# A table that moves 40 operations in the planned issue order of a two-stage conditioned block, and four PSUM banks for the last quarter turned by TensorE

## The chip, the core and the metric

The kernel runs on one core of one Trainium2 chip. The metric is the device time of one launch in microseconds (us). TensorE is called PE in the profile, its weight loads PEld, VectorE is DVE, ScalarE is ACT, GpSimd is POOL and SyncE is SP; here they are named either way.

## The reference, cut to what matters

`x` has 2 x 2048 tokens of 512 features, all in float32. A condition vector gives six modulation vectors, which scale and shift two normalisations and gate two branches:

```python
emb = silu(t) @ ada_w + ada_b
shift_msa, scale_msa, gate_msa, shift_mlp, scale_mlp, gate_mlp = split(emb, 6)
h = gelu((_ln(x) * (1 + scale_msa) + shift_msa) @ ssm_w1 + ssm_b1)        # 512 -> 512, exact gelu
x = x + gate_msa * (h @ ssm_w2 + ssm_b2)                                  # 512 -> 512
hf = gelu((_ln(x) * (1 + scale_mlp) + shift_mlp) @ ff_w1 + ff_b1)         # 512 -> 1024, tanh gelu
return x + gate_mlp * (hf @ ff_w2 + ff_b2)                                # 1024 -> 512
```

## The kernel before

**Tiles and stages.** The 4096 tokens are cut into eight blocks of 512 (`TB`). Each block goes through `norm1`, `ssm1`, `ssm2` and `norm2`; the last of these sends the normalised tokens, turned so that features lie on partitions, through DRAM (`turned_d`). Then four pairs of blocks go through the two products of the second branch, `up` (stage names "ff1 0" to "ff1 3") and `down` ("ff2 0" to "ff2 3").

**Fewer multiplications.** Each product is done by a scheme with seven multiplications of halves instead of eight, with sums of operands made beforehand (`first`, `second`) and sums of results behind. `up` and `down` use it twice, one inside the other: seven outer products of seven inner ones, so 49 multiplications, called leaves here. A leaf of `down` is two matmuls with 256 columns, and each of these is two records of the trace, so a leaf is four. The price of fewer matmuls is adds: operand sums between SBUF tiles on VectorE or GpSimd (`parts` calls `tt("vg", ...)`, line 258), and results added out of PSUM on VectorE (line 258 too, or `scaled_add`, line 1049).

**Banks.** PSUM has eight banks. Inside one inner product the leaves run in the order P1, P5, P6, P2, P7, P3, P4 (`CARRIED`). P1, P6, P7 and P4 write into one bank in turn, so P7 can't begin before VectorE has read what P6 left there. Two inner products are interleaved, leaf by leaf, so there are three other leaves between P6 and P7 of one product.

**What sets the order.** Nothing is issued while the functions run. Each operation is recorded with `Plan.add` (line 67): the engines that may do it (`engs`, where "vg" lets VectorE or GpSimd do it), an assumed cost, and in `shared` the engines on which it takes what the planner treats as one shared lock, a port between SBUF and these two engines. An add between SBUF tiles takes it on either engine; an add with a PSUM operand takes it on GpSimd only; copies, transposes and statistics of VectorE don't take it. `Plan.order` (line 89) works out by when each result is due if TensorE is never to wait, and `simulate` (line 113) runs a list schedule: of the operations that could start now on an engine the one that is due first is taken, and where several engines could start at the same time the one that is due first goes. The kernel then issues everything in the order of the simulated starts, so each engine's instructions stand in a fixed order in the program.

**Port waits.** Where the simulation shows that GpSimd was ready, but VectorE held the lock, the GpSimd operation gets `after` (lines 180 and 181), and line 1405 turns this into a real dependency: on the chip GpSimd then waits until that VectorE operation has ended. It is the planner's way to let an urgent VectorE add go first.

**DMAs.** All are issued by SP's queue, some by ScalarE's. They take eight completion semaphores in turn, in the order of issue, so that a DMA can't be issued before the eighth one ahead of it has landed.

**The end.** The last two outer products of the last pair finish two quarters of the output. TensorE turns them back to token rows (`turned_by_pe`, line 1187): for each of four parts of a quarter two transposes go into a PSUM bank (line 306), VectorE adds the kept input out of that bank (line 1201), and a DMA writes the part out. `TURNED_AT` (line 1184) gives each half `h` of a quarter `blk` a bank; the two parts `e` of a half share it.

Of the kernel before, what the change touches and what calls it, by code (L numbers as in the profile page):

```python
# [13 lines left out]
EPS = 1e-06  # L14


class Op:
    __slots__ = ("n", "engs", "fn", "cost", "lat", "shared", "size", "lead", "care", "after", "done", "sooner", "deps", "succ", "late", "on", "start", "end", "note")


class Plan:
# [67 lines left out]
    def order(self):  # L89
        ops = self.ops  # L90
        for op in ops:
            if op.engs == "p":
                op.deps = {d for d in op.deps if ops[d].engs != "p"}
            for d in op.deps:
                ops[d].succ.append(op.n)
        t, due = 0.0, {}
        for op in ops:
            if op.engs == "p":
                due[op.n] = t
                t += op.cost["p"]  # L100
        due.update((n, t + late) for n, late in self.closing)
        for _ in range(2):
            for op in reversed(ops):
                late = due.get(op.n, 1e9)
                for s in op.succ:
                    late = min(late, ops[s].late - (1 + op.care) * (self.HOP + min(op.lat.values()) + op.size / self.RATE))
                op.late = late - op.sooner
            self.simulate()
            wait = ops[self.anchor].start - due[self.anchor]
            due = {n: t + wait for n, t in due.items()}  # L110
        return sorted(ops, key=lambda op: (op.start, op.n))

    def simulate(self):
        ops, hop = self.ops, self.HOP
# [86 lines left out]
def kernel(  # L201
# [51 lines left out]
    def tt(e, o, a, b, f):  # L253
        n, ps = cols(o), in_psum(a, b)
        cost = {"v": n / 0.96 + 70, "g": 2.12 * n + 145}
        plan.add(
            e,
            lambda E: E.tensor_tensor(o, a, b, f),  # L258
            [o],
            [a, b],  # L260
            cost,
            {"v": cost["v"] + 85, "g": cost["g"] + 45},
            "g" if ps else "vg",
        )
# [38 lines left out]
    def turn_by_pe(o, a, identity, start, stop):  # L303
        plan.add(
            "p",
            lambda E: E.matmul(o, a, identity, start=start, stop=stop, is_transpose=True, skip_group_check=True),  # L306
            [o],
            [a, identity],
            {"p": 120.0},
            {"p": 290.0},  # L310
        )

    def dma(o, a, q="s", lead=0.0, lat=2000.0, sooner=0.0):
        size = max(cols(o.unsqueeze(0)), 1) * 4
        outs = [o] if o.tensor.name in scratch else []
        ins = [a] if a.tensor.name in scratch else []
        lead = lead or (0.0 if ins or not outs or size <= plan.LITTLE else 25000.0)
        plan.add(q, lambda E: E.dma_start(out=o, in_=a), outs, ins, {q: plan.ISSUE}, {q: lat}, size=size, lead=lead)
        plan.ops[-1].sooner = sooner
# [24 lines left out]
    def kb(t, at, n):  # L344
        return t[:, at * 256 : (at + n) * 256]

    def cut(t, form, **sizes):
        return t.rearrange(form, **sizes)
# [5 lines left out]
    banks = []  # L354
# [40 lines left out]
    ident = kb(far_r, 24, 1)[:, :P]  # L395
# [548 lines left out]
    summed = cut(rows_r, "p (r e t) -> p r e t", r=4, e=2)  # L944
# [115 lines left out]
    def rest_in(s, d, blk, x):  # L1060
        half = slice(d * D // 2, (d + 1) * D // 2)
        dma(x, x1_d[2 * s + blk][:, :, half])
        return x, out_blk[2 * s + blk][:, :, half]
# [117 lines left out]

        return sums, last_sum, prepare, leaf

    TURNED_AT = ((3, 4), (2, 0))
    tail, waiting, leaves_read = [{}, {}], [], [0]

    def turned_by_pe(blk, r, f, quad):
        got = tail[blk]
        if not got:
            got["x"], got["out"] = rest_in(NBLK // 2 - 1, 1, blk, cut(kb(hidden_r, 8 * blk, 4), "p (c d) -> p c d", c=C))  # L1190

        def turned_back():
            e, h = int(quad[0]) - 1, int(quad[1]) - 1
            bank = cut(banks[TURNED_AT[blk][h]], "p (c e d) -> p c e d", c=2, e=2)
            for c in range(2):
                col = slice((2 * h + c) * P, (2 * h + c + 1) * P)
                turn_by_pe(bank[:, c, e], summed[:, r, e, col], ident, c == 0 and h not in got, c == 1)
            got[h] = True
            c, d = slice(2 * h, 2 * h + 2), slice(e * P, (e + 1) * P)
            x = got["x"][:, c, d]  # L1200
            tt("v", x, bank[:, :, e], x, ALU.add)
            dma(got["out"][:, c, d], x, "sa"[e])
            plan.closing.append((plan.ops[-1].n, 3000.0))

        n = leaves_read[0] = leaves_read[0] + 1
        if f in ("P7", "P2", "P3", "P4"):
            waiting.append((n, turned_back))
        done = blk == 0 and f == "P4"
        while waiting and (done or waiting[0][0] + 2 <= n):
            waiting.pop(0)[1]()  # L1210
# [190 lines left out]
    behind = mybir.DependencyInfo(mybir.DependencyClass.Sync, mybir.DependencyReason.DATA)  # L1401
# [49 lines left out]
```

## Time and profile before

| | |
|---|---|
| time, median of 3 runs | 562.89 us (562.89, 562.89, 564.47) |
| the profiled execution: its own time / its span | 563.11 us / 561.3 us |
| PE busy | 552.9 us, 98% of the span |
| PEld busy | 481.7 us, 86% |
| DVE busy | 479.2 us, 85% |
| POOL busy | 385.0 us, 69% |
| ACT busy | 282.9 us, 50% |
| granted TensorE clock | 0.998 |
| HBM traffic | 217 GB/s over the span |

The span runs from the first instruction of the program to the last end. In rows of a timeline the first number is the start in us from there, the second the duration, then engine, line of the source, operation, output and inputs, the shape, and a count where equal neighbours are merged; in brackets stands how long the engine had been idle and what ended that. Lines 296 and 306 are the matmul and the transpose of TensorE; 258 is every add. Since one helper records all adds, tiles tell them apart: `rows<-bank,rows` adds a leaf's result out of PSUM, `far`, `near`, `hidden`, `turned`, `fw` are regions of SBUF that hold operands and their sums.

### The profile page before, as it was taken

The numbers are of one execution on the slowest core, as the hardware profiler recorded it, in microseconds if no ns is written. First come the engines' busy times: TensorE is split into PE (matmuls) and PEld (weight loads), VectorE is DVE, ScalarE is ACT, GpSimd is POOL, SyncE is SP. The second block draws the span as 40 slices with busy tenths as digits, with TensorE's granted clock in tenths as the row PEclk, the third lists the DMA queues.
The fourth block names the chain that finished last, engine by engine and source line by source line (L and its number), as shares of the span: only waits on it lengthen the run. The fifth ranks groups of instructions, "written<-read, shape, count | busy, mean of one in ns | idle before, by whom it ended". The sixth has DMA issues, their size and how long they took to land.

```text
span 561.3 us, 8747 instructions
## 1 busy us (share of the span) xinstructions
PE 552.9 (98%) x2809; PEld 481.7 (86%) x2809; DVE 479.2 (85%) x848; ACT 282.9 (50%) x523; POOL 385.0 (69%) x475
## 2 busy tenths in 40 slices
PE   8999999999999999999999999999999999999995
PEld 4888889888898988888888888888888888888884
DVE  5696888888779578899999997789988989998987
ACT  3473866674877844666205347414247414244230
POOL 2887747979946299985646868676767766547581
PEclk9999999999999999999999999999999999999999
DMA  8963799988399978995201999611998612983417
GB/s 313 398 229 82 233 363 309 316 259 269 106 276 327 291 311 249 330 292 171 57 20 38 286 322 301 226 39 45 303 325 286 212 39 67 312 288 122 140 45 218
DMA packets 66945, 123.68 MB, mean 220 GB/s; under 512 B 5668, under 2 KB 34260, under 8 KB 65364
## 3 DMA queue, kind: packets, MB, share of 16 engines
q1 hardware_dynamic: 64080, 121.27, 65.9%
q10 hardware_dynamic: 2820, 1.86, 1.3%
q8 instruction: 22, 0.36, 0.3%
q14 instruction: 23, 0.19, 0.1%
HBM read 77.89 MB, written 44.18 MB: 217 GB/s over the span
## 4 chain that ended last, share of the span: by engine, by line
PE 91%; DVE 6%; DMA 2%; POOL 0%; issue 0%; DVEq 0%; POOLq 0%
PE bank L296 90%; DVE rows L258 2%; DVE near L258 1%; DMA fw<-in_L_cond_ada_w_dram 1%; DVE far L258 1%; PE bank L306 1%; DVE fw L258 1%; DVE hidden L258 0%; DMA fw<-in_L_cond_ada_b_dram 0%; DVE far L1073 0%; POOL far L258 0%; POOL fw L258 0%; POOL rows L258 0%; DVE turned L660 0%; DVE rows L1049 0%
## 5 line engine op out<-in xcount | busy, mean ns | idle before, releaser
L296 PE MATMUL bank<-turned,ring 128*128 128x256 f32 x896 | 210.2, 380 | 0.2 <-DVE turned L660 0.2
L296 PEld LDWEIGHTS bank<-turned,ring 128*128 128x128 f32 x896 | 168.0, 190 | 23.1 <-DVE turned L660 0.4
L258 DVE TENSOR_TENSOR hidden<-bank,hidden 128x512 f32<-128x512 f32 (+2 forms) x178 | 126.4, 738 | 23.9 <-PE bank L296 19.9
L296 PE MATMUL bank<-near,hidden 128*128 128x256 f32 (+1 forms) x470 | 95.1, 350 | 0.0
L296 PEld LDWEIGHTS bank<-near,hidden 128*128 128x128 f32 x470 | 82.2, 191 | 9.3 <-POOL near L258 0.3
L296 PE MATMUL bank<-far,fw 128*128 128x256 f32 (+1 forms) x354 | 86.0, 374 | 0.2
L258 POOL TENSOR_TENSOR turned<-turned 128x512 f32<-128x512 f32 (+1 forms) x62 | 70.4, 1148 | 20.4 <-DVE turned L258 9.0
L296 PE MATMUL bank<-ring 128*128 128x256 f32 x336 | 82.4, 380 | 0.0
L258 DVE TENSOR_TENSOR rows<-bank,rows 128x256 f32<-128x256 f32 (+1 forms) x142 | 66.1, 478 | 16.0 <-PE bank L296 11.9
L296 PEld LDWEIGHTS bank<-far,fw 128*128 128x128 f32 x354 | 66.5, 190 | 9.6 <-issue 0.5
L296 PEld LDWEIGHTS bank<-ring 128*128 128x128 f32 x336 | 63.7, 190 | 9.0 <-issue 0.5
L285 ACT COPY bank<-bank 128x512 f32<-128x512 f32 (+2 forms) x84 | 37.7, 449 | 63.0 <-PE bank L296 62.2
L276 ACT ACTIVATE hidden<-hidden,cols 128x512 f32<-128x512 f32 (+1 forms) x66 | 44.7, 710 | 42.9 <-DVE hidden L258 42.9
L258 POOL TENSOR_TENSOR hidden<-hidden 128x128 f32<-128x128 f32 (+2 forms) x45 | 43.5, 976 | 25.3 <-DVE hidden L258 13.1
L296 PE MATMUL bank<-near,fw 128*128 128x256 f32 (+1 forms) x246 | 60.7, 377 | 0.0
L296 PE MATMUL bank<-hidden,fw 128*128 128x256 f32 (+1 forms) x216 | 53.3, 376 | 0.4 <-DVE rows L258 0.4
L296 PEld LDWEIGHTS bank<-near,fw 128*128 128x128 f32 x246 | 46.1, 190 | 6.4 <-issue 0.2
L276 ACT ACTIVATE turned<-turned,mod,mod 128x512 f32<-128x512 f32 x56 | 42.2, 807 | 9.0 <-DMA turned<-turned 8.4
L296 PEld LDWEIGHTS bank<-hidden,fw 128*128 128x128 f32 x216 | 40.3, 190 | 6.5 <-DVE rows L258 0.8
L258 POOL TENSOR_TENSOR ring<-turned,ring 128x256 f32<-128x256 f32 x42 | 30.6, 740 | 20.7 <-PE bank L296 17.0
L276 ACT ACTIVATE rows<-rows,gb,mod 128x512 f32<-128x512 f32 (+1 forms) x34 | 26.5, 787 | 34.9 <-DVE rows L258 25.0
L258 POOL TENSOR_TENSOR fw<-fw 128x256 f32<-128x256 f32 (+1 forms) x38 | 35.6, 944 | 11.8 <-DMA fw_parts<-fw 4.3
(123 smaller groups left out, 735.7 us busy)
## 6 DMA issues: line engine op xcount, KB each, us to landing
ring<-fw_parts SPq DMA_DIRECT2D x28, 512.0 KB, 4.8
turned<-far SPq DMA_DIRECT2D x52, 256.0 KB, 4.2
ring<-fw_parts SPq DMA_DIRECT2D x28, 384.0 KB, 5.2
turned<-turned SPq DMA_DIRECT2D x32, 256.0 KB, 5.4
back<-far SPq DMA_DIRECT2D x52, 128.0 KB, 2.9
rows<-back SPq DMA_DIRECT2D x13, 512.0 KB, 5.1
fw_parts<-fw SPq DMA_DIRECT2D x21, 256.0 KB, 4.6
fw<-in_L_cond_ada_w_dram SPq DMA_DIRECT2D x5, 1024.0 KB
```

The costliest lines, as they stand in the source:

```text
L258: lambda E: E.tensor_tensor(o, a, b, f),
L276: lambda E: E.activation(o, a, func, bias=bias, scale=scale),
L285: plan.add("a", lambda E: E.copy(o, a), [o], [a], {"a": cost}, {"a": cost + 60})
L296: lambda E: E.matmul(o, lhsT, rhs, start=start, stop=stop, skip_group_check=True, **kw),
L306: lambda E: E.matmul(o, a, identity, start=start, stop=stop, is_transpose=True, skip_group_check=True),
```

## The change

**A table.** `MOVED` holds 40 triples: an operation's number, an engine, and the number of the operation behind which it now stands on that engine. 32 stand on VectorE or GpSimd, five on ScalarE (two of these are DMAs) and three on SP. Ten of the operations change between VectorE and GpSimd.

**A second pass.** After the last `simulate`, a new method `in_lines` takes the five lines of operations as simulated, takes out the moved ones and puts each at its new place. Then it runs all lines strictly in order with the planner's costs, which gives new starts, and it sets every operation's `after` anew. At each step it takes the line whose head can start first; that one head is due sooner than another plays no part any more. `after` is set where, in these new starts, VectorE held the lock when GpSimd was ready.

```diff
+MOVED = (
+    (229, "v", 217), (230, "v", 242), (644, "v", 1420), (653, "v", 645), (1241, "v", 1445), (1745, "v", 1753),
...
+    (3531, "a", 3550), (3535, "a", 3527), (221, "g", 250), (646, "g", 1287), (662, "g", 1516), (2013, "g", 2301),
...
-        return sorted(ops, key=lambda op: (op.start, op.n))
+        self.in_lines()
+        return sorted(ops, key=lambda op: (op.start, op.turn))
+
+    def in_lines(self):
+        ops, moved = self.ops, {n for n, _, _ in MOVED}
+        lines = {e: [] for e in "pvags"}
+        for op in sorted(ops, key=lambda op: (op.start, op.n)):
+            if op.n not in moved:
+                lines[op.on].append(op)
+        for n, e, behind in MOVED:
+            at = next((k + 1 for k, op in enumerate(lines[e]) if op.n == behind), 0)
+            lines[e].insert(at, ops[n])
...
+        for turn in range(len(ops)):
+            soon = []
+            for e in "pavgs":
+                if at[e] < len(lines[e]) and not left[lines[e][at[e]].n]:
+                    op = lines[e][at[e]]
+                    start = max(free[e], ready[op.n], lanes[0] if op.size else lock if e in op.shared else 0.0)
+                    soon.append((start, "pavgs".index(e), e, op))
+            start, _, e, op = min(soon)
+            op.on, op.start, op.turn, op.after = e, start, turn, None
...
+            if e in op.shared:
+                if e == "g" and holder and holder.on == "v" and start > max(free_at, ready[op.n]):
+                    op.after = holder
+                lock, holder = start + op.cost[e], op
...
-    TURNED_AT = ((3, 4), (2, 0))
+    TURNED_AT = (((3, 0), (2, 4)), ((2, 2), (0, 0)))
...
-            bank = cut(banks[TURNED_AT[blk][h]], "p (c e d) -> p c e d", c=2, e=2)
+            bank = cut(banks[TURNED_AT[blk][h][e]], "p (c e d) -> p c e d", c=2, e=2)
...
-                turn_by_pe(bank[:, c, e], summed[:, r, e, col], ident, c == 0 and h not in got, c == 1)
+                turn_by_pe(bank[:, c, e], summed[:, r, e, col], ident, c == 0 and (not blk or h not in got), c == 1)
```

**The banks.** Each of the four parts of the quarter that is finished last (`blk` 0) now has a bank of its own; the other quarter keeps its two.

What the program's order shows of this follows at three places. The names are those of tiles, with numbers of PSUM banks (72 to 79); the line of every add is 258 before and 309 after, because the new code stands above it. In brackets stand the semaphores that an instruction waits for: `DVE_49` counts ends of VectorE's instructions, `PE_49`, `Pool_49` and `Activation_49` those of the others, `DMAHW0_49` to `DMAHW7_49` landings of DMAs. TensorE's order is the same up to the banks of the last two pairs of transposes.

**GpSimd in the fourth `norm2`** (`marks` are its small statistics, `fw` an operand sum of the weights of `up`, `turned` an operand sum of `norm1`). Before:

```order
L568 TENSOR_TENSOR marks_129<-marks_129 128x4 [waits Pool_49]
L569 TENSOR_SCALAR marks_129<-marks_129 128x4 [waits DVE_49,Pool_49]
L570 TENSOR_TENSOR marks_129<-marks_129 128x4 [waits DVE_49,Pool_49]
L258 TENSOR_TENSOR fw_71<-fw_71 128x256 [waits DMAHW6_49,DMAHW1_49]
L571 TENSOR_TENSOR marks_129<-marks_129 128x4 [waits Pool_49]
L572 TENSOR_SCALAR marks_129<-marks_129 128x4 [waits DVE_49,Pool_49]
L258 TENSOR_TENSOR turned<-turned 128x512 [waits DMAHW0_49,Activation_49]
L258 TENSOR_TENSOR turned<-turned 128x4x2x64 [waits DVE_49]
L258 TENSOR_TENSOR turned<-turned 128x512
L258 TENSOR_TENSOR fw_71<-fw_71 128x256 [waits DMAHW5_49]
```

and after:

```order
L619 TENSOR_TENSOR marks_129<-marks_129 128x4 [waits Pool_49]
L620 TENSOR_SCALAR marks_129<-marks_129 128x4 [waits DVE_49,Pool_49]
L621 TENSOR_TENSOR marks_129<-marks_129 128x4 [waits Pool_49]
L309 TENSOR_TENSOR fw_71<-fw_71 128x256 [waits DMAHW5_49]
L309 TENSOR_TENSOR fw_71<-fw_71 128x256 [waits DMAHW6_49,DMAHW1_49,DVE_49]
L622 TENSOR_TENSOR marks_129<-marks_129 128x4 [waits Pool_49]
L623 TENSOR_SCALAR marks_129<-marks_129 128x4 [waits Pool_49]
L309 TENSOR_TENSOR turned<-turned 128x512 [waits DMAHW0_49,Activation_49]
```

The `fw` add that waits for `DMAHW5_49` (operation 646, which overwrites what a DMA sends to `fw_parts`) stood behind three `turned` adds and now stands ahead of the last two steps of the statistics.

**VectorE in the first `down`** ("ff2 0"). Before:

```order
L258 TENSOR_TENSOR near<-hidden,near 128x1024
L258 TENSOR_TENSOR rows<-bank_78,rows 128x256 [waits PE_49]
L258 TENSOR_TENSOR rows<-bank_77,rows 128x256
L258 TENSOR_TENSOR rows<-bank_73,rows 128x256 [waits PE_49]
L258 TENSOR_TENSOR fw_71<-fw_71 128x2x128
L258 TENSOR_TENSOR near<-hidden,near 128x1024
L258 TENSOR_TENSOR rows<-bank_79,rows 128x256 [waits DVE_49,PE_49]
L258 TENSOR_TENSOR rows<-rows 128x256 [waits DVE_49]
L258 TENSOR_TENSOR rows<-bank_74,rows 128x2x256 [waits DVE_49,PE_49]
```

and after:

```order
L309 TENSOR_TENSOR near<-hidden,near 128x1024
L309 TENSOR_TENSOR far<-near,far 128x512
L309 TENSOR_TENSOR fw_71<-fw_71 128x256
L309 TENSOR_TENSOR rows<-bank_78,rows 128x256 [waits PE_49]
L309 TENSOR_TENSOR rows<-bank_77,rows 128x256
L309 TENSOR_TENSOR rows<-bank_73,rows 128x256 [waits PE_49]
L309 TENSOR_TENSOR fw_71<-fw_71 128x2x128
L309 TENSOR_TENSOR rows<-bank_79,rows 128x256 [waits DVE_49,PE_49]
L309 TENSOR_TENSOR near<-hidden,near 128x1024
L309 TENSOR_TENSOR rows<-rows 128x256 [waits DVE_49]
L309 TENSOR_TENSOR rows<-bank_74,rows 128x2x256 [waits DVE_49,PE_49]
```

One `fw` add stands earlier, and the second `near` add of 1024 elements has changed places with the read of bank 79. GpSimd's next `far<-near` add had `after` the `rows<-rows` add and now has it after the `fw_71` add of 128x2x128.

**GpSimd and VectorE in the second `down`** ("ff2 1"). GpSimd before:

```order
L258 TENSOR_TENSOR far<-hidden,far 128x512 [waits DVE_49,PE_49]
L258 TENSOR_TENSOR far<-near,far 128x512
L258 TENSOR_TENSOR near<-near 128x512 [waits Pool_49]
L258 TENSOR_TENSOR hidden<-hidden 128x1024 [waits DVE_49]
L258 TENSOR_TENSOR hidden<-hidden 128x1024 [waits DVE_49,Pool_49]
L258 TENSOR_TENSOR far<-near,far 128x512 [waits DVE_49,PE_49]
L258 TENSOR_TENSOR near<-hidden,near 128x1024 [waits DVE_49,PE_49]
L258 TENSOR_TENSOR near<-hidden,near 128x1024 [waits DVE_49]
```

and after:

```order
L309 TENSOR_TENSOR far<-hidden,far 128x512 [waits PE_49,Pool_49]
L309 TENSOR_TENSOR far<-near,far 128x512 [waits DVE_49]
L309 TENSOR_TENSOR near<-near 128x512 [waits Pool_49]
L309 TENSOR_TENSOR hidden<-hidden 128x1024
L309 TENSOR_TENSOR hidden<-hidden 128x1024 [waits DVE_49,Pool_49]
L309 TENSOR_TENSOR far<-near,far 128x512 [waits DVE_49,PE_49,Pool_49]
L309 TENSOR_TENSOR near<-hidden,near 128x1024 [waits DVE_49]
```

The first `hidden` add of 1024 elements no longer waits for VectorE, nor does the first `far` add; the second `hidden` add still does, but its `after` has gone one VectorE operation ahead (from `near<-near` to the second `far<-near,far`). One `near` add has left GpSimd. VectorE before, at the same place:

```order
L258 TENSOR_TENSOR far<-hidden 128x512 [waits Pool_49]
L258 TENSOR_TENSOR rows<-bank_74,rows 128x256 [waits DVE_49,PE_49]
L258 TENSOR_TENSOR rows<-bank_79,rows 128x256 [waits DVE_49,PE_49]
L258 TENSOR_TENSOR far<-hidden,far 128x512 [waits Pool_49]
L258 TENSOR_TENSOR rows<-bank_76,rows 128x256 [waits PE_49]
```

and after:

```order
L309 TENSOR_TENSOR far<-hidden 128x512 [waits Pool_49]
L309 TENSOR_TENSOR far<-hidden,far 128x512 [waits DVE_49,Pool_49]
L309 TENSOR_TENSOR rows<-bank_74,rows 128x256 [waits DVE_49,PE_49]
L309 TENSOR_TENSOR rows<-bank_79,rows 128x256 [waits DVE_49,PE_49]
L309 TENSOR_TENSOR rows<-bank_76,rows 128x256 [waits PE_49]
L309 TENSOR_TENSOR near<-hidden,near 128x1024
```

The `far<-hidden,far` add has gone ahead of two bank reads, and the `near` add that left GpSimd stands here. GpSimd's last `near` add has `after` the first of these rows, `far<-hidden`.

More of the change, by code (lines that the diff above doesn't have):

```diff
@@ L14 @@
 EPS = 1e-06
+MOVED = (
[7 rows of a table added]
+)
 class Op:
-    __slots__ = ("n", "engs", "fn", "cost", "lat", "shared", "size", "lead", "care", "after", "done", "sooner", "deps", "succ", "late", "on", "start", "end", "note")
+    __slots__ = ("n", "engs", "fn", "cost", "lat", "shared", "size", "lead", "care", "after", "done", "sooner", "deps", "succ", "late", "on", "start", "end", "note", "turn")
 class Plan:
@@ L110, in order @@
             due = {n: t + wait for n, t in due.items()}
-        return sorted(ops, key=lambda op: (op.start, op.n))
+        self.in_lines()
[9 more added lines that the diff above has]
+            lines[e].insert(at, ops[n])
+        left, ready = [len(op.deps) for op in ops], [0.0] * len(ops)
+        free, at = dict.fromkeys("pvags", 0.0), dict.fromkeys("pvags", 0)
+        lock, pipe, holder, lanes = 0.0, 0.0, None, [0.0] * self.LANES
+        for turn in range(len(ops)):
[7 more added lines that the diff above has]
+            op.on, op.start, op.turn, op.after = e, start, turn, None
+            free_at, free[e] = free[e], start + op.cost[e]
+            at[e] += 1
+            if op.size > self.LITTLE:
+                pipe = max(start + self.FLIGHT, pipe) + op.size / self.RATE
+                op.end = pipe + self.LANDING
+            else:
+                op.end = start + op.lat[e]
+            if op.size:
+                lanes = sorted(lanes[1:] + [op.end])
+            if e in op.shared:
+                if e == "g" and holder and holder.on == "v" and start > max(free_at, ready[op.n]):
+                    op.after = holder
+                lock, holder = start + op.cost[e], op
+            for n in op.succ:
+                gap = 0.0 if ops[n].engs == e and not op.size else self.HOP
+                ready[n] = max(ready[n], op.end + gap)
+                left[n] -= 1
     def simulate(self):
```

5 rows, old and new, of the table MOVED are left out of this document.

## Prediction

> **What bounds the kernel now.** I read the page's busy times first, then its chain, then TensorE's waits, then timelines of the stages in which the change moves something.
>
> ```profile
> PE 552.9 (98%) x2809; PEld 481.7 (86%) x2809; DVE 479.2 (85%) x848; ACT 282.9 (50%) x523; POOL 385.0 (69%) x475
> ...
> PE 91%; DVE 6%; DMA 2%; POOL 0%; issue 0%; DVEq 0%; POOLq 0%
> ```
>
> PE is busy for 98% of the span and is 91% of the chain. The matmuls don't change, so the change can only add to or take from the idle places between them. All that it can win inside is small, while a queue that now feeds PE late costs as much as it is late. So I go through the places one by one: which read of a bank or copy stands just ahead of a PE row, and how early. A leaf takes 0.86 us (rows of PE start 0.86 apart for each four matmuls), and a leaf behind a wait shows 1.10 to 1.13 instead of 1.03, so each wait costs 0.1 more.
>
> **Second `down` ("ff2 1"): two adds of GpSimd let go.** GpSimd, VectorE and PE there:
>
> ```profile
> 353.39 1.27 POOL L258 TENSOR_TENSOR far<-hidden,far 128x512 f32<-128x512 f32 x1 [1.83 <-DVE near L258]
> ...
> 355.84 1.28 POOL L258 TENSOR_TENSOR near<-near 128x512 f32<-128x512 f32 x1
> 358.95 2.36 POOL L258 TENSOR_TENSOR hidden<-hidden 128x1024 f32<-128x1024 f32 x1 [1.83 <-DVE far L258]
> 361.99 2.35 POOL L258 TENSOR_TENSOR hidden<-hidden 128x1024 f32<-128x1024 f32 x1 [0.69 <-DVE near L258]
> ```
> ```profile
> 356.65 1.02 DVE L258 TENSOR_TENSOR far<-near 128x512 f32<-128x512 f32 x1
> 357.59 1.28 DVE L258 TENSOR_TENSOR far<-near,far 128x512 f32<-128x512 f32 x2
> 358.79 0.41 DVE L258 TENSOR_TENSOR rows<-bank,rows 128x256 f32<-128x256 f32 x1
> ...
> 360.78 1.07 DVE L258 TENSOR_TENSOR near<-near 128x512 f32<-128x512 f32 x1
> 361.77 0.41 DVE L258 TENSOR_TENSOR rows<-bank,rows 128x256 f32<-128x256 f32 x1
> ...
> 363.37 1.52 DVE L258 TENSOR_TENSOR far<-hidden 128x512 f32<-128x512 f32 x1
> 364.81 0.41 DVE L258 TENSOR_TENSOR rows<-bank,rows 128x256 f32<-128x256 f32 x1
> ```
> ```profile
> 360.24 1.89 PE L296 MATMUL bank<-far,fw 128*128 128x256 f32 x8
> 361.97 2.75 PE L296 MATMUL bank<-near,fw 128*128 128x256 f32 x12
> ...
> 366.28 1.89 PE L296 MATMUL bank<-far,fw 128*128 128x256 f32 x8
> ```
>
> The rows show the lock at work. VectorE's `far<-hidden` takes 1.52 instead of some 0.65: it ends at 364.89, 0.55 after GpSimd's add (361.99 + 2.35 = 364.34). The waits in brackets are the other side: GpSimd is held until a named VectorE add has ended.
>
> The Trainium skill (page "SBUF — State Buffer", section "Who interferes with whom") says that the one that issues first has the shared pair for its whole instruction and the other is fully blocked. By it a blocked add would end a full 0.68 after GpSimd, each wait below would grow by 0.13 or so and the sum would be 565.7; the row's 0.55 speaks for a little overlap, and I go by the row.
>
> The first `hidden` add no longer waits 1.83, so it stands behind `near<-near` from 357.1. VectorE's `far<-near` is already waiting and ends at 357.67; then GpSimd has the lock until about 359.9. The first `far<-near,far` ends at 360.45 instead of 358.23, the second at 361.05, and the bank read at 361.45 instead of 359.20. The leaf into that bank is the second of the PE row of 360.24, at 361.10, and a matmul starts a little behind the read that it waits for: **0.4 late**. The second `hidden` add now follows VectorE's second `far<-near,far`, from 361.1 to 363.5, so `near<-near` ends at 364.05 instead of 361.85 and the next bank read at 364.4; its leaf is the third of the row of 361.97, at 363.69 and with the first wait (0.4 and 0.1) 364.2: **0.3 late**. Then `far<-hidden`, behind GpSimd's next add of 1.27, ends at about 365.97. At that end two instructions are let go: GpSimd's `near` add of 1024 elements (2.35) and VectorE's moved `far<-hidden,far`, which now stands ahead of the bank read of 364.81. Who is first is read from another place:
>
> ```profile
> 284.30 1.21 DVE L258 TENSOR_TENSOR near<-hidden,near 128x1024 f32<-128x1024 f32 x1
> ...
> 286.43 0.71 DVE L258 TENSOR_TENSOR fw<-fw 128x256 f32<-128x256 f32 x1
> 287.06 1.21 DVE L258 TENSOR_TENSOR near<-hidden,near 128x1024 f32<-128x1024 f32 x1
> 288.20 0.41 DVE L258 TENSOR_TENSOR rows<-bank,rows 128x256 f32<-128x256 f32 x1
> 288.64 0.43 DVE L258 TENSOR_TENSOR rows<-rows 128x256 f32<-128x256 f32 x1
> 289.18 1.02 DVE L258 TENSOR_TENSOR rows<-bank,rows 128x512 f32<-128x512 f32 x2
> ```
> ```profile
> 285.59 1.27 POOL L258 TENSOR_TENSOR hidden<-hidden 128x512 f32<-128x512 f32 x1 [2.10 <-DVE near L258]
> 289.21 1.27 POOL L258 TENSOR_TENSOR far<-near 128x512 f32<-128x512 f32 x1 [2.36 <-DVE rows L258]
> ```
> ```profile
> 290.01 1.10 PE L296 MATMUL bank<-hidden,fw 128*128 128x256 f32 x4
> 291.25 1.10 PE L296 MATMUL bank<-far,fw 128*128 128x256 f32 x4
> ...
> 293.32 2.00 PE L296 MATMUL bank<-far,fw 128*128 128x256 f32 x8
> ```
>
> GpSimd with one wait starts 0.08 after VectorE's end (285.51 to 285.59); VectorE with two waits, one for its own last instruction, 0.11 after it (289.07 to 289.18). The GpSimd add has one wait, the VectorE add two, so GpSimd is first by 0.03, until 368.4; VectorE ends at 368.95 and the read at 369.3. Its leaf is the second of the row of 366.28, at 367.15, and with 0.9 of the two waits 368.05: **1.3 late**. In all 2.0 and three times 0.1: **+2.3**. PE's rows there have no idle time now, so nothing can be won; the bounds are 0 and 2.8 (0.55 taken as 0.68, and the reads 0.1 later).
>
> **First `down` ("ff2 0"): +0.5.** The rows above. GpSimd's `far<-near` waited 2.36 for `rows<-rows`; now it follows the `fw` add that ends at 287.14, from about 287.25 to 288.52, and VectorE's `near` add of 1024, now behind the read of bank 79, ends at 289.6 instead of 288.27. `rows<-rows` ends at 290.07 and the first of the next two reads at 290.87 instead of 289.87. The leaf of 290.01 waits for it; it waits 0.18 today, and 0.87 more then. The wait ahead of 291.25 (0.38) goes, since its `fw` add stands earlier; that ahead of 293.32 (0.27) stays. So 0.87 - 0.4 = 0.5. Bounds: all three waits go, -0.8; none goes and one grows, with the third, to +1.3. I take the middle, worked out row by row.
>
> **Fourth `norm2`: +0.4.** GpSimd takes the `fw` add of operation 646 ahead of the last steps of the statistics:
>
> ```profile
> 165.55 0.73 POOL L258 TENSOR_TENSOR fw<-fw 128x256 f32<-128x256 f32 x1 [4.26 <-DMA fw_parts<-fw]
> ...
> 172.94 0.73 POOL L258 TENSOR_TENSOR fw<-fw 128x256 f32<-128x256 f32 x1
> ...
> 179.01 1.59 POOL L258 TENSOR_TENSOR fw<-fw 128x256 f32<-128x256 f32 x2
> ```
> ```profile
> 168.60 7.61 SPq L318 DMA_DIRECT2D fw_parts<-fw  x8
> ```
> ```profile
> fw_parts<-fw SPq DMA_DIRECT2D x12, 256.0 KB, 4.6
> ...
> turned<-turned SPq DMA_DIRECT2D x4, 256.0 KB, 7.1
> ```
> ```profile
> 178.88 0.38 ACT L285 COPY bank<-ring 128x256 f32<-128x256 f32 x1
> ```
> ```profile
> 180.71 0.39 PE L296 MATMUL bank<-near,hidden 128*128 128x128 f32 x2
> ```
>
> The add now waits for a DMA of SP's row of 168.60. Landing 4.6 after issue it is there at 173.2, with 7.1 at 175.7; GpSimd is at the place at 172.94, so it waits 0.2 to 2.7 and the add takes 0.8. All behind it, the statistics that ScalarE's normalisation needs among it, is 1.0 to 3.5 later. ScalarE's copy ends 1.4 ahead of the matmul at 180.71, and one ScalarE operation of 0.8 that is moved ahead fills part of its wait. What is left for PE is 0 to 1.3; by the median landing nothing, by the late one 1.3, and the add that waited 4.26 in this stage says that late ones are had: 0.4, a third of the way.
>
> The Trainium skill (page "DMA: Bandwidth & Descriptors", section "Anatomy of one DMA — SWDGE (gpsimd) path") fits 2.0 us and bytes at 436 GB/s, which would be an estimated 2.6 for 256 KB; the add would then find its data, this term would be 0 and the sum 564.8. The measured 4.6 speaks against it here, on SP's queue.
>
> **Small gains.**
>
> ```profile
> 33.03 3.10 PEld L296 LDWEIGHTS bank<-near,hidden 128*128 128x128 f32 x15 [0.27 <-POOL near L258]
> ```
> ```profile
> 460.23 1.02 DVE L258 TENSOR_TENSOR rows<-bank,rows 128x512 f32<-128x512 f32 x2 [1.22 <-POOL rows L258]
> ```
> ```profile
> 460.98 1.13 PE L296 MATMUL bank<-hidden,fw 128*128 128x256 f32 x4 [0.40 <-DVE rows L258]
> ```
> ```profile
> 555.70 0.66 PE L306 MATMUL bank<-far,rows 128*128 128x128 f32 x4 [0.69 <-DVE hidden L258]
> ```
> ```profile
> 556.18 0.76 DVE L258 TENSOR_TENSOR hidden<-bank,hidden 128x256 f32<-128x256 f32 x2 [0.53 <-PE bank L306]
> ```
>
> At 33.0 a `near` add goes to VectorE, and the wait of 0.27 with it: **-0.3**, bounds 0 and -0.4. At 460.98 the `rows<-rows` add that VectorE's read waited 1.22 for is moved from GpSimd to VectorE; of 0.40 and the longer leaf I take **-0.3**, bounds 0 and -0.6. At the end the last four transposes wait for VectorE's `hidden` add, which reads the bank that they share; with banks of their own that add and the two of 556.18 follow each other, from 555.64: 0.54 earlier, and so are the last writes: **-0.5**, bounds 0 and -0.7. The other moves stand where no PE row has idle time. Three DMAs of SP's queue and two of ScalarE's pass one to four neighbours each, at some 0.95 per issue by the row of 168.60 (7.61 for eight); what they bring is needed a whole leaf sequence later, and landings of 4.6 to 7.1 lie between, so a delay of two or three issues hides there. I cost them and the remaining adds at nothing, and 0.5 either way if that cover is gone.
>
> **The sum.** 2.3 + 0.5 + 0.4 - 0.3 - 0.3 - 0.5 = +2.1. The profiled execution took 563.1 (its span 561.3 and 1.8 around it), 0.2 above the median of 562.89. So 565.2; the terms' own spread makes it 564.6 to 566.0.
>
> **Rivals.** *A, faster:* GpSimd's first `far` add (353.39) also loses its wait of 1.83. If its short adds come over 1 us earlier, its 1024 add starts before 356.3 and is through before VectorE's adds of 357.59; then all the waits of "ff2 1" are absent, and with the gains at their best (0.8 in "ff2 0", 0.3, 0.6, 0.5, norm2 0) it is 560.9. Against it: the second `far` add now waits for VectorE's `near` add, which would itself be held by the earlier GpSimd add, so little is gained. 0.13. *B:* VectorE is first at the pair that is 0.03 apart. The 1.3 and 0.1 go: 563.8. Both gaps are of single rows; 0.17. *C:* the DMA of norm2 is late (1.3) and the wait ahead of 291.25 stays: 565.2 + 0.9 + 0.4 = 566.5. 0.13. *D:* the change does not act where I see costs, since other waits keep the old order; the three gains alone give 562.0. 0.05.
>
> **Chances.** My forecast has 0.50; 0.02 is left for gains that I don't see. The measurement can tell about 0.3%, 1.7 us, from no change, so faster means under 561.2 and slower over 564.6. Faster: A and the rest, 0.15. Same: B and D, 0.22. Slower: the forecast and C, 0.63. The range 561.6 to 566.6 takes in B, C and D, and leaves out A.
>
> **What the profile after would show.** GpSimd's two `hidden` adds of 1024 at about 357.1 and 361.1; VectorE's first `far<-near,far` 2 us long; three gaps of PE between 361 and 370, the third over 1 us; one gap of about 1 us near 290, and no wait at 33.0 nor at the last transposes; a DMA wait of GpSimd near 173. I am wrong if PE runs gapless through "ff2 1", if the third gap is missing (B), or if a gap over 0.5 us stands in a place not named here.

## The result and the profile after

The changed kernel takes 566.95 us (median of six runs, 566.19 to 569.44); the kernel before 563.20 (six runs). The ratio is 1.0074, with a 95% interval of 1.0063 to 1.0085: **3.7 us slower**, where +2.1 was forecast. The profiled execution took 568.29, its span 566.5, so it is 1.3 above the median; its gaps are read below for their places, and what a part of the change costs is taken from medians where an experiment gives one.

The page: busy times and the chain of the changed kernel.

```profile
PE 554.4 (98%) x2809; PEld 480.5 (85%) x2809; DVE 482.3 (85%) x852; ACT 283.1 (50%) x523; POOL 380.3 (67%) x471
...
PE 84%; DVE 7%; POOL 3%; issue 2%; DMA 2%; ACT 1%; DVEq 0%; POOLq 0%; ACTq 0%
```

PE's share of the chain has fallen from 91% to 84%; GpSimd and ScalarE are on it now. Since TensorE's order is the same, the start of the same PE row in both timelines says where the time went:

| row of PE starts at, before | after | after is late by | what lies between |
|---|---|---|---|
| 33.03 | 32.87 | -0.2 | the `near` add moved to VectorE |
| 177.25 | 177.42 | 0.2 | waits at 82 and 86, 0.4 in all, which no other profile shows |
| 181.60 | 183.24 | 1.6 | fourth `norm2` |
| 288.96 | 291.76 | 2.8 | waits at 205 and 216 |
| 295.15 | 298.81 | 3.7 | "ff2 0" |
| 353.33 | 356.95 | 3.6 | nothing |
| 368.01 | 374.20 | 6.2 | "ff2 1" |
| 460.98 | 466.59 | 5.6 | the `rows<-rows` add moved to VectorE |
| end of the span 561.3 | 566.5 | 5.2 | the four banks |

**"ff2 1"**, in this order GpSimd, VectorE and PE. GpSimd is no longer held, and VectorE's adds are long:

```profile
355.49 1.73 POOL L309 TENSOR_TENSOR far<-hidden,far 128x512 f32<-128x512 f32 x1
...
360.85 2.84 POOL L309 TENSOR_TENSOR hidden<-hidden 128x1024 f32<-128x1024 f32 x1
364.99 2.35 POOL L309 TENSOR_TENSOR hidden<-hidden 128x1024 f32<-128x1024 f32 x1 [1.29 <-DVE far L309]
...
369.95 2.35 POOL L309 TENSOR_TENSOR near<-hidden,near 128x1024 f32<-128x1024 f32 x1 [0.63 <-DVE far L309]
```
```profile
356.01 2.29 DVE L309 TENSOR_TENSOR near<-hidden,near 128x1024 f32<-128x1024 f32 x1
...
361.39 3.45 DVE L309 TENSOR_TENSOR far<-near,far 128x512 f32<-128x512 f32 x2
364.76 0.41 DVE L309 TENSOR_TENSOR rows<-bank,rows 128x256 f32<-128x256 f32 x1
...
369.97 2.87 DVE L309 TENSOR_TENSOR far<-hidden,far 128x512 f32<-128x512 f32 x1
372.77 1.27 DVE L309 TENSOR_TENSOR rows<-bank,rows 128x256 f32<-128x256 f32 x3
```
```profile
365.23 1.13 PE L347 MATMUL bank<-far,fw 128*128 128x256 f32 x4 [0.22 <-DVE rows L309]
...
368.37 1.10 PE L347 MATMUL bank<-near,fw 128*128 128x256 f32 x4 [0.28 <-DVE rows L309]
...
373.23 1.13 PE L347 MATMUL bank<-far,fw 128*128 128x256 f32 x4 [1.17 <-DVE rows L309]
```

Against the same rows of before PE loses 0.39, 0.44 and 1.41 there, the longer leaves aside: the three waits of the forecast. At 369.95 and 369.97 GpSimd and VectorE start 0.02 apart; GpSimd is first, and VectorE's add ends 0.54 after it (372.84 against 372.30).

**"ff2 0"**: GpSimd's add at 289.95 is 0.1 ahead of VectorE's, which so takes 2.24 instead of 1.21, and PE waits three times (rows of GpSimd, VectorE and PE).

```profile
289.95 1.27 POOL L309 TENSOR_TENSOR far<-near 128x512 f32<-128x512 f32 x1 [0.42 <-DVE fw L309]
```
```profile
290.06 2.24 DVE L309 TENSOR_TENSOR near<-hidden,near 128x1024 f32<-128x1024 f32 x1
...
292.74 1.02 DVE L309 TENSOR_TENSOR rows<-bank,rows 128x512 f32<-128x512 f32 x2
```
```profile
293.57 1.10 PE L347 MATMUL bank<-hidden,fw 128*128 128x256 f32 x4 [0.79 <-POOL fw L309]
...
296.51 1.10 PE L347 MATMUL bank<-far,fw 128*128 128x256 f32 x4
297.84 1.13 PE L347 MATMUL bank<-far,fw 128*128 128x256 f32 x4 [0.23 <-DVE far L309]
```

By the starts of its rows, the longer leaf aside, PE waits 0.95 ahead of 293.57, 0.27 ahead of 296.51, as it did before the change ahead of 293.32, and 0.39 ahead of 297.84, where it did not. The first row names GpSimd's `fw` add, but the kernel before (290.01, with the add at 291.18) and E8 start this leaf ahead of that add. What it waits for is the first of the two bank reads at 292.74 (0.69 long): it ends 0.15 ahead of the leaf, as it did before the change.

**Fourth `norm2`**: GpSimd at operation 646, then ScalarE, then PE. "Fourth" is the number in the kernel, where blocks are counted from 0 (`norm2 4`). Operation 1704 scales and shifts tokens of block 0 that come back from DRAM for `up` (`tokens 0`); it now stands ahead of the last such operation of block 7's `norm1`.

```profile
176.86 1.41 POOL L309 TENSOR_TENSOR fw<-fw 128x256 f32<-128x256 f32 x2 [3.46 <-DMA fw_parts<-fw]
```
```profile
176.55 1.52 ACT L327 ACTIVATE turned<-turned,mod,mod 128x512 f32<-128x512 f32 x2 [1.41 <-DMA turned<-turned]
178.78 0.81 ACT L327 ACTIVATE near<-fw,marks 128x512 f32<-128x512 f32 x1 [0.71 <-POOL marks L623]
...
201.67 1.52 ACT L327 ACTIVATE turned<-turned,mod,mod 128x512 f32<-128x512 f32 x2 [3.41 <-DMA turned<-turned]
```
```profile
180.04 1.99 PE L347 MATMUL bank<-turned,ring 128*128 128x256 f32 x8 [0.72 <-POOL turned L309]
182.25 0.49 PE L347 MATMUL bank<-near,hidden 128*128 128x128 f32 x2 [0.21 <-ACT bank L336]
...
206.54 8.90 PE L347 MATMUL bank<-near,hidden 128*128 128x256 f32 x40 [0.51 <-ACT bank L336]
```

GpSimd waited 3.46 for the DMA that 646 needs, more than the 2.7 taken as the most. ScalarE waited too, 1.41, at a place where it did not wait before; the first of the two operations of that row is 1704, moved ahead. PE then waits for a `turned` add of GpSimd and for ScalarE's copy, and once more at 206.54.

**The end**: PE's last six transposes run as one row, where the last four waited 0.69, and VectorE's last three adds follow each other.

```profile
560.31 1.18 PE L357 MATMUL bank<-far,rows 128*128 128x128 f32 x6
```
```profile
560.91 1.08 DVE L309 TENSOR_TENSOR hidden<-bank,hidden 128x256 f32<-128x256 f32 x3
```

### The profile page after: what moved, and what is told of

It is laid out like the page before. It is cut to its first block, busy times and chain, and to the rows that moved or that the text cites. A ratio compares the mean times of both kernels' runs of the same rounds, so it can differ in the third digit from the quotient of the medians.

```text
span 566.5 us, 8739 instructions
## 1 busy us (share of the span) xinstructions
PE 554.4 (98%) x2809; PEld 480.5 (85%) x2809; DVE 482.3 (85%) x852; ACT 283.1 (50%) x523; POOL 380.3 (67%) x471
## 4 chain that ended last, share of the span: by engine, by line
PE 84%; DVE 7%; POOL 3%; issue 2%; DMA 2%; ACT 1%; DVEq 0%; POOLq 0%; ACTq 0%
PE bank L347 84%; DVE far L309 2%; DVE rows L309 2%; DMA fw<-in_L_cond_ada_w_dram 1%; POOL turned L309 1%; DVE near L309 1%; DVE hidden L309 1%; DVE fw L309 1%; PE bank L357 1%; POOL fw L309 1%; POOL marks L611 0%; DMA fw<-in_L_cond_ada_b_dram 0%; ACT near L327 0%; DVE far L1124 0%; ACT bank L336 0%
## 5 line engine op out<-in xcount | busy, mean ns | idle before, releaser
L309 POOL TENSOR_TENSOR ring<-turned,ring 128x256 f32<-128x256 f32 x39 | 28.3, 732 | 24.0 <-PE bank L347 18.4
```

## The experiments

Each changes the one thing shown; times are medians with the ratio to the kernel before, which took 563.20 beside the first four and 563.23 beside the others.

**E1: operation 646 left in place.**

```diff
-    (221, "g", 250), (646, "g", 1287), (662, "g", 1516), (2013, "g", 2301),
+    (221, "g", 250), (662, "g", 1516), (2013, "g", 2301),
```

> The changed kernel, with operation 646 left at its old place on GpSimd, behind the turned adds. Between the two profiles PE falls 1.5 us further behind at the fourth norm2 and 1.2 us more at 204 and 213 us, and GpSimd waited 3.46 us for that operation's DMA. Theory 1 (all of this follows from that one wait): 2.7 us less than the changed kernel's 566.95, so about 564.3, and no gaps of PE at 179, 181, 205 and 216. Theory 2 (the term was sized rightly at 0.4, and the rest is another profile's luck with DMAs, or the ScalarE moves): 566.5, and the gaps at 205 and 216 stay. Theory 3 (the direct 1.5 is of 646, the later 1.2 of other moves): 565.4.

566.69 (1.0056, 1.0043 to 1.0070): nearly nothing, and theory 1 falls as it stood. PE is on time at 179 and only 0.2 late at 181, but it loses another 1.1 and 0.5 at 205 and 216. The time and these two gaps are those of theory 2, which left open whether they come from DMAs that happened to land late or from ScalarE's moves. ScalarE and GpSimd show more:

```profile
175.96 1.52 ACT L327 ACTIVATE turned<-turned,mod,mod 128x512 f32<-128x512 f32 x2 [1.58 <-DMA turned<-turned]
...
200.83 1.52 ACT L327 ACTIVATE turned<-turned,mod,mod 128x512 f32<-128x512 f32 x2 [3.75 <-DMA turned<-turned]
```
```profile
177.62 1.27 POOL L309 TENSOR_TENSOR turned<-turned 128x512 f32<-128x512 f32 x1 [1.36 <-ACT turned L327]
```

Operation 1704 waits 1.58 for a landing at the head of ScalarE's queue. Behind it stand the last `turned` of `norm1`, for which GpSimd waits, and the normalisation of the fourth `norm2`. So that block's normalised tokens still go out late. The 3.75 are not a wait for these, but for tokens of block 1 (`tokens 1`), sent out some 70 us earlier: SP's queue issues the four reads that bring them back behind the four late writes. The reads are issued 2.3 later than before, and ScalarE starts 3.2 later (200.83 against 197.66). The writes (`turned<-far`) and the reads, in the kernel before and in E1:

```profile
182.05 3.48 SPq L318 DMA_DIRECT2D turned<-far  x4
...
190.08 2.10 SPq L318 DMA_DIRECT2D turned<-turned  x4
```
```profile
185.63 3.59 SPq L369 DMA_DIRECT2D turned<-far  x4
...
192.34 2.41 SPq L369 DMA_DIRECT2D turned<-turned  x4
```

Another theory was needed: two waits side by side.

**E2: "ff2 1" as before.** Operations 2528 and 2544 back, and six of the nine port waits that the change altered there as before. Of the edit, without the lines that turn `HOLD` into dependencies:

```diff
-    ... (2303, "v", 2318), (2544, "v", 2543), (2528, "v", 2532),
+    ... (2303, "v", 2318),
...
+HOLD = {2425: 2516, 2426: 2517, 2455: 2424, 2518: 2543, 2528: 2544, 2529: 2545}
...
-            op.on, op.start, op.turn, op.after = e, start, turn, None
+            op.on, op.start, op.turn, op.after = e, start, turn, ops[HOLD[op.n]] if op.n in HOLD else None
```

> The changed kernel, with the second down as before: operations 2528 and 2544 at their old places, and GpSimd's adds there held behind the same VectorE adds as before. Theory 1 (the three waits of PE in that stage, 0.39, 0.44 and 1.41 with 0.1 each and 0.18 ahead of them, are the change's, and nothing later takes their place): 2.6 us less than 566.95, so 564.3, and PE without gaps between 358 and 374. Rival (the lateness is partly absorbed further on, or a wait downstream takes over): 565.5.

564.30 (1.0019, 1.0010 to 1.0028), 2.65 less than the changed kernel, as theory 1 has it. The rows of PE where the three waits were:

```profile
361.55 1.89 PE L347 MATMUL bank<-far,fw 128*128 128x256 f32 x8
363.28 2.75 PE L347 MATMUL bank<-near,fw 128*128 128x256 f32 x12
...
367.59 1.89 PE L347 MATMUL bank<-far,fw 128*128 128x256 f32 x8
```

No row has idle time ahead of it, and eight or twelve matmuls merge into one row, as before the change.

**E3: an empty table**, so the old order with the port waits set anew and the four banks.

```diff
 MOVED = (
-    (229, "v", 217), (230, "v", 242), (644, "v", 1420), (653, "v", 645), (1241, "v", 1445), (1745, "v", 1753),
...
 )
```

> The changed kernel with an empty table: every line of operations as before, but the port waits set anew by the second pass, and the four banks at the end. It tells the second pass apart from the moves. Theory 1 (the two hidden adds of 1024 elements that GpSimd is no longer held for cost two of the three waits in the second down; the third is the moved far add's): two gaps of about 0.4 near 361 and 364, none of 1.3, a gap of about 1 us near 290, the old waits at 33, 461 stay; 563.2 + 0.2 + 1.0 + 0.9 - 0.6 = 564.7. Rival (the port waits alone change nothing, the moves cost all): the banks' gain only, 562.6.

564.41 (1.0020, 1.0011 to 1.0030); theory 1 said 564.7. The runs lie between 564.17 and 564.75. Every engine has the order of E4, so that puts 1.7 us on the port waits set anew, with no operation moved (the order between the two DMA queues differs at five places as well). In the profiles 0.7 of it falls in "ff2 0", 0.8 in "ff2 1" and 0.25 at 392. PE in "ff2 0" and "ff2 1":

```profile
291.05 1.10 PE L347 MATMUL bank<-hidden,fw 128*128 128x256 f32 x4 [0.98 <-POOL fw L309]
...
295.20 1.13 PE L347 MATMUL bank<-far,fw 128*128 128x256 f32 x4 [0.33 <-DVE far L309]
```
```profile
365.14 1.10 PE L347 MATMUL bank<-near,fw 128*128 128x256 f32 x4 [0.28 <-DVE rows L309]
```

The gap near 290 is there, and the second wait of "ff2 1"; the first is small (0.13) and the third absent, which needs the moved `far` add.

**E4: the kernel before with the four banks.**

```diff
-    TURNED_AT = ((3, 4), (2, 0))
+    TURNED_AT = (((3, 0), (2, 4)), ((2, 2), (0, 0)))
...
```

> The kernel before with the four banks at the end, and nothing else. Theory 1 (the last transposes no longer wait for the add that reads the shared bank): PE's last gap of 0.85 shrinks to about 0.3 and the end comes 0.5 earlier, 562.7. Rival (the end is set by the last landings of DMAs, which do not care): 563.2.

562.74 (0.9993, 0.9984 to 1.0002): 0.46 less by the medians, the interval reaching just over no change. The last transposes merge into one row here as well, so theory 1 is the likelier.

```profile
554.78 1.18 PE L306 MATMUL bank<-far,rows 128*128 128x128 f32 x6
```

**E5: operation 1704 left in place**, 646 moved.

```diff
-    (3202, "v", 3196), (3246, "v", 3336), (3428, "v", 3564), (1704, "a", 1238), (1706, "a", 1705), (1522, "a", 1706),
+    (3202, "v", 3196), (3246, "v", 3336), (3428, "v", 3564), (1706, "a", 1705), (1522, "a", 1706),
```

> The changed kernel, with ScalarE's operation 1704 (a normalisation of turned tokens of the next block, which needs four DMAs) left behind the fourth norm1's last one; 646 stays moved. Leaving 646 alone in place gave 566.69, nearly nothing, and there ScalarE waited 1.58 us for a DMA at 176 and GpSimd's third turned add 2 us. Theory 1 (two waits side by side: 646 on GpSimd and 1704 on ScalarE each hold the same normalisation, so that either alone is enough): 566.3, PE still 1.5 late at 179 and 181. Theory 2 (1704 is the whole cost, 646 is hidden): 564.3. Theory 3 (neither; the later 1.2 are of the luck of DMAs): 566.9, and gaps of another size.

567.78 (1.0079, 1.0066 to 1.0092): no better than the changed kernel. GpSimd, ScalarE and PE:

```profile
176.31 1.41 POOL L309 TENSOR_TENSOR fw<-fw 128x256 f32<-128x256 f32 x2 [3.31 <-DMA fw_parts<-fw]
```
```profile
178.22 0.81 ACT L327 ACTIVATE near<-fw,marks 128x512 f32<-128x512 f32 x1 [2.78 <-POOL marks L623]
```
```profile
182.40 0.49 PE L347 MATMUL bank<-near,hidden 128*128 128x128 f32 x2 [0.92 <-ACT bank L336]
```

ScalarE's queue no longer stops at 1704, and it waits 2.78 for GpSimd's statistics instead: theory 2 is out. The time is 1.5 above the 566.3 of theory 1, and the runs don't show why. In this profile PE loses 2.0 at 179 and 182 and nothing at 205 and 216.

**E6: both left in place.**

```diff
-    (3202, "v", 3196), (3246, "v", 3336), (3428, "v", 3564), (1704, "a", 1238), (1706, "a", 1705), (1522, "a", 1706),
-    (3531, "a", 3550), (3535, "a", 3527), (221, "g", 250), (646, "g", 1287), (662, "g", 1516), (2013, "g", 2301),
+    (3202, "v", 3196), (3246, "v", 3336), (3428, "v", 3564), (1706, "a", 1705), (1522, "a", 1706),
+    (3531, "a", 3550), (3535, "a", 3527), (221, "g", 250), (662, "g", 1516), (2013, "g", 2301),
```

> The changed kernel with 646 and 1704 both at their old places. Theory 1 (two waits side by side): the whole 2.7 of this stage and the two behind it goes, 564.3, no gap of PE between 178 and 217 over 0.2, and the spread of the runs shrinks from over 3 us to under 1. Theory 2: as with 1704 alone. Theory 3: 566.5.

565.66 (1.0041, 1.0029 to 1.0054), and the runs lie within 0.7 us (565.20 to 565.88) instead of 3.3. Two waits side by side are borne out; ScalarE's normalisation starts at once and PE's rows join:

```profile
174.99 0.81 ACT L327 ACTIVATE near<-fw,marks 128x512 f32<-128x512 f32 x1
```
```profile
177.02 3.62 PE L347 MATMUL bank<-turned,ring 128*128 128x256 f32 x16
180.47 0.38 PE L347 MATMUL bank<-near,hidden 128*128 128x128 f32 x2
```

The gain is 1.3 and not 2.7, since 2.7 was read from an execution 1.3 above its median. The waits at 205 and 216 are gone as well, with all other moves of that stretch kept: ScalarE waits 1.40 for the tokens of block 1 here, where it waited 3.41 and 3.75. The landing still varies with both in place. In the profile of E8 that wait is 2.61, and PE loses 0.4 at 214, at the row that is at 216 in the others.

**E7: E6, and GpSimd's `near` add held behind VectorE's moved `far` add.** On top of E6 one entry; the lines that read it are those of E2:

```diff
+HOLD = {2529: 2544}
...
```

> As the one before (646 and 1704 in place), and one more wait: GpSimd's near add of 1024 elements in the second down is held until VectorE's moved far add has ended, where both were let go by the same end. Theory 1 (that add's 2.35 ahead of VectorE's far add and bank read is the third wait of that stage, and only who is first decides): the third gap of PE, 1.4 us with the longer leaf, goes, the first two stay; 1.4 us under the one before. Rival (the far add in front of the bank read is late by itself, with or without GpSimd): a gap of over 0.5 stays.

564.16 (1.0016, 1.0008 to 1.0025), 1.5 less than E6. GpSimd, VectorE and PE:

```profile
367.35 2.35 POOL L309 TENSOR_TENSOR near<-hidden,near 128x1024 f32<-128x1024 f32 x1 [1.42 <-DVE far L309]
```
```profile
366.58 0.69 DVE L309 TENSOR_TENSOR far<-hidden,far 128x512 f32<-128x512 f32 x1
```
```profile
367.64 1.89 PE L347 MATMUL bank<-far,fw 128*128 128x256 f32 x8
```

VectorE's add takes 0.69 instead of 2.87, and PE's third gap is gone; a small one, 0.2 with its longer leaf, comes ahead of 371.18. A wait added makes the kernel faster; who goes first was the whole of that term.

**E8: the changed kernel without the costs found.** E2 and E6 together, and GpSimd's `far<-near` add of "ff2 0" held behind `rows<-rows` as before.

```diff
+HOLD = {2425: 2516, 2426: 2517, 2455: 2424, 2518: 2543, 2528: 2544, 2529: 2545, 2112: 2088}
...
```

> The changed kernel without what the runs so far show as costs: 646, 1704, 2528 and 2544 at their old places, the second down's port waits as before, and in the first down GpSimd's far add held behind the rows<-rows add as before. Left are the banks, the other moves and the other port waits. Theory 1 (terms add up): 566.95 - 2.7 - 2.6 - 0.8 = 560.9, under the kernel before by 2.3, no gap of PE over 0.5 besides those at the start. Rival (what is taken away in one place comes back in the next wait, as with 646 alone): 562.5 or more.

561.58 (0.9970, 0.9959 to 0.9982): **faster than both**, by 1.7 than the kernel before, where adding the terms gave 560.9. GpSimd, VectorE and PE in "ff2 0":

```profile
289.13 1.27 POOL L309 TENSOR_TENSOR far<-near 128x512 f32<-128x512 f32 x1 [2.23 <-DVE rows L309]
```
```profile
287.44 1.21 DVE L309 TENSOR_TENSOR near<-hidden,near 128x1024 f32<-128x1024 f32 x1
```
```profile
290.00 1.03 PE L347 MATMUL bank<-hidden,fw 128*128 128x256 f32 x4
290.87 1.03 PE L347 MATMUL bank<-far,fw 128*128 128x256 f32 x4
```

With GpSimd held 2.23 again, two of that stage's three old waits are gone and the third is small: its moves gain 0.8 there, where the new port wait had made them a loss of 0.9. That 560.9 is so near is partly luck. The sum took 2.7 for the fourth `norm2`, where E6 gives 1.3, and in "ff2 0" it took back the loss of 0.8 but did not count the gain of 0.8. With both put right it is some 561.5.

## Why the prediction was off

The direction and most mechanisms held; the size did not.

- **"ff2 1", +2.3 forecast.** Right, a little small: E2 measures 2.65. GpSimd's two adds stand at 360.85 and 364.99, or 357.2 and 361.4 when the 3.6 of the table is taken off, where 357.1 and 361.1 were forecast; the three gaps of 0.4, 0.3 and 1.3 measured 0.39, 0.44 and 1.41. VectorE's first `far<-near,far` takes 2.85; the "2 us long" of the forecast does not fit its own ends (357.6 to 360.45). The race was forecast 0.03 in GpSimd's favour and was 0.02; E7 shows that it decides. What was missed is a fourth wait, ahead of the three: GpSimd's first `far` add (355.49), let go too, holds up VectorE's `near` add of 1024 (2.29 for 1.21) and the bank read behind it. The prediction saw this in rival A, where it spoke against a gain, and did not count it as a cost: 0.2 in this profile, 0.3 to 0.6 in E1, E5 and E6, and none in E7, whose order is the same up to there.
- **The rule of the Trainium skill** (page "SBUF — State Buffer", section "Who interferes with whom") that the first to issue has the pair and the other blocks: the traces agree on who wins, down to 0.02 us, and E7 turns the outcome by turning the order. They differ on the length: the blocked add ended 0.54 behind, not the full 0.69 that it takes alone in E7.
- **"ff2 0", +0.5.** Between the two profiles +0.9. The leaf of 290 waited 0.95 (worked out: 1.05), the wait ahead of 291.25 went and that ahead of 293.32 stayed at 0.27, all as forecast. What the sum lacked is the new wait of 0.39 one leaf later, for a `far` add of VectorE, whose adds come late behind the long `near` add.
- **Fourth `norm2`, +0.4.** The step that failed. By medians it is 1.3 (E6). In single executions it varies: the changed kernel's profile loses 2.6 there, that of E2, with the same moves at that place, 0.8. Four things were wrong. The landing for 646 was put a third of the way from the median (4.6 after issue) to the late one (7.1); the add that waited for it started 6.7, 7.1 and 6.5 after SP's issue in the profiles of the changed kernel, E5 and E2. "One ScalarE operation of 0.8 that is moved ahead fills part of its wait": that operation, 1704, itself needs four landings and waited 1.41 and 1.58 with the whole queue behind it. The price was worked out for one queue, so that taking 646 back alone gained little (E1), 1704 alone nothing (E5), and only both the whole (E6). And the price was followed to the next matmul only: the block's late writes hold up the reads behind them in SP's queue, and ScalarE's wait for these (3.41 and 3.75 us) costs PE again at 205 and 216. The forecast's own sign of being wrong came there: a gap over 0.5 in a place that it does not name (0.51 at 206.54). The sentence from the Trainium skill (page "DMA: Bandwidth & Descriptors", section "Anatomy of one DMA — SWDGE (gpsimd) path"), by which 646 would have found its data, is not borne out on SP's queue: GpSimd waited 3.31 and 3.46.
- **The small gains.** 33.0: -0.3 with its shorter leaf, as forecast. 460.98: -0.57 (-0.3 forecast), the whole wait, where PE comes late; -0.3 in E2 and E8. The banks: -0.46 in E4 (-0.5).
- **The sum.** With 2.65, 0.9, 1.3, -0.3, -0.6 and -0.5 it is 3.45, near the measured 3.7. Rival C (566.5) was the nearest: its late DMA came, its second condition, that the wait ahead of 291.25 stays, did not. A, B and D did not come.

## What to carry to other kernels

An operation that is moved forward on a queue brings its own inputs' lateness with it: before counting it as filler, look up when its DMA lands, on every engine that the table touches, and which reads would stand behind late writes in the DMA queue. Undoing one of two waits that run side by side shows nothing, so take both away before calling either harmless. An added wait can be worth more than a removed one where two engines share a resource: E7's single wait is worth 1.5 us, and the port waits set anew, without any move, cost 1.7.

## What the runs showed of the hardware that was not expected

The spread of the runs goes with the waits for DMAs. With 646 and 1704 moved the six runs lie within 3.3 us (566.19 to 569.44) and those of E2 within 2.1; with one of them moved within 2.4 (E1) and 1.6 (E5); with both in place within 0.7 (E6), 0.8 (E7) and 0.5 (E8). The same wait of GpSimd for 646's landing is 3.46, 3.31 and 2.88 us in the profiles of the changed kernel, E5 and E2, so landings that vary from run to run are the likely reason: in these kernels they end waits that PE sees. That was not measured run by run.
